# RWKV6 in a four-layer hybrid: the value rows reach all keys by transfers from DRAM, not by matmuls

## The chip, the cores and the metric

The kernel runs on one core of a Trainium2 chip. The metric is the time of one execution on the device, in microseconds (us); lower is better. All data are float32.

## What is computed

The input x is 4 sequences of 1024 tokens with 256 channels. Four residual layers follow one another, each on a layer norm of x: a retention layer, a mixture of experts (8 experts, 2 for each token), an RWKV6 layer, and the same mixture of experts again. The change is in the RWKV6 layer, cut here to its core (16 heads of 16 channels; `r_`, `k_`, `v_`, `w_` are projections of token-shifted mixes of x):

```python
ww = time_decay + jnp.tanh(xw @ td_w1) @ td_w2
w = jnp.exp(-jnp.exp(ww))
def step(state, rkvw):
    r_t, k_t, v_t, w_t = rkvw
    a = k_t[..., :, None] * v_t[..., None, :]
    y = jnp.einsum('bhk,bhkv->bhv', r_t, state + u[None, :, :, None] * a)
    new_state = w_t[..., :, None] * state + a
    return (new_state, y)
_, ys = jax.lax.scan(step, state0, (r_, k_, v_, w_))
# then: norm of y within each head, times silu(xg @ Wg), times Wo, added to x
```

## The kernel before

**Stages.** From 0 to about 350 us retention runs together with the start of the first routing, to about 672 us the tiles of the first mixture of experts (two halves of the tokens, 39 tiles each), from 686.8 to 1345 us the RWKV6 loop, and then the tiles of the second mixture. The orders of TensorE, ScalarE, VectorE and GpSimd in and after the loop are those of the program, written out by hand; the order of SP, which issues nearly all plain transfers, comes from a scheduler.

**The loop.** A block is 512 tokens; there are eight, and two blocks in a row make one sequence. Channels lie on partitions, tokens along the free axis, so that the recurrence over tokens is one scan instruction. The 256 channels are two groups g of 128 partitions (8 heads x 16 keys). The state of a head is 16 keys x 16 values; each scan handles one value index for all keys of a group. `step(j, n, ...)` treats block j and step n from 0 to 7, where n stands for g and a quarter i of the value indices (g, i = divmod(n, 4)); a step makes two runs, h = 0 and 1, of two value indices q each. "Run (n, h)" below means that one.

A run, before:
- `fill` (L916): two products on TensorE with a 0/1 matrix `pick` copy v of each head to the partitions of its 16 keys, into the PSUM tile `w_vb` (two buffers).
- `run`: VectorE multiplies `w_vb` by k in place (L939, 128x1024), then makes two scans (L941, 128x512) with w from `w_wT`, into `w_s` (six buffers). Between the two scans stand single VectorE instructions of other work: `root`, `gated`, `added`, `bonus` for neighbouring blocks, and `m.biased` (L506) of the second mixture's router. GpSimd then multiplies `w_s` by r (L949).
- `sums` (L972), one step later: TensorE adds up over the keys; after four steps ScalarE copies the result (L977).

Around the runs stand, by hand-written tables (`amid`, `late`, `uses`, `given`): the preparation of the next block (`mix`, `deltas` with its products L841 and its mixes on VectorE L851 or GpSimd L854 and L855, `decay`, `decay2`, `projected`), and the norm, gate and output of the block before. At the end of step 0 of blocks 2 to 7 the router's logits for a finished block follow (`logits`: four ScalarE instructions L487, transposes, products L502), and L506 takes them in the middle of run (1, 0). Block 5 also has the routing itself (L528 to L633), blocks 6 and 7 the sends of routed rows (L641, GpSimd's indirect transfers). In blocks 0 and 1 `join` (L759) adds the first mixture's results to x.

At step 1 of the last block all expert weights of the second mixture are loaded into the room that the RWKV6 inputs leave (`load_w1`, `load_w2`, L1228 and L1234; 16 transfers).

Of the kernel before, what the change touches and what calls it, by code (L numbers as in the profile page):

```python
# [36 lines left out]
F32 = mybir.dt.float32  # L37
I32 = mybir.dt.int32
AF = mybir.ActivationFunctionType
# [43 lines left out]

O_PICK = 0
O_SEL = O_PICK + 4 * P
O_SUM = O_SEL + 4 * 32
# [17 lines left out]
def hybrid_kernel(  # L104
# [670 lines left out]
    def rwkv(pi, w):  # L775

        st = [dict() for _ in range(NBLK)]

        def half(where, name, bufs=2):
# [86 lines left out]
        def decay2(j):  # L868

            d = st[j]  # L870
            wT = d["wT"] = full(pcs, "w_wT")
            for m in range(KC):
                wp = psum([P, BLK], "w_wp")
                mm(wp, lhsT=w["td_w2"][:, m * P : (m + 1) * P], rhs=d["tw"][:64, :],
                   start=True, stop=True)
                ew = half(pi, "w_ew", 1)
                nc.scalar.activation(ew, wp, AF.Exp, bias=vec[:, m, V_DECAY : V_DECAY + 1])
                nc.scalar.activation(wT[:, m, :], ew, AF.Exp, scale=-1.0)

        def projected(j, n, f):  # L880
            d = st[j]
            o = d[n] = full(pct if n == "g" else pcs, f"w_{n}T")
            for m in range(KC):
                pp = psum([P, BLK], "w_pp")
                for c in range(KC):
                    mm(pp, lhsT=w[n][:, c, m * P : (m + 1) * P], rhs=d["xf", f][:, c, :],
                       start=(c == 0), stop=(c == KC - 1))
                if n == "g":
                    nc.scalar.activation(o[:, m, :], pp, AF.Silu)
                else:  # L890
                    nc.scalar.copy(o[:, m, :], pp)
# [15 lines left out]

        def fill(j, n, h, among=()):


            d = st[j]
            g, i = divmod(n, 4)
            vb = d["vb", n, h] = pvb.tile([P, 2, BLK], F32, name="w_vb", tag="w_vb", bufs=2)
            for q in range(2):
                rows = slice(32 * (2 * h + q), 32 * (2 * h + q) + 32)
                mm(vb[:, q, :], lhsT=w["pick"][rows, i, :], rhs=d["v"][rows, g, :],  # L916
                   start=True, stop=True)
                for f in among[q::2]:
                    f()

# [12 lines left out]
        def run(j, n, h, between=()):  # L933


            d = st[j]
            g, i = divmod(n, 4)
            vb, s = d["vb", n, h], d["s", n, h]
            nc.vector.tensor_mul(vb, vb, d["k"][:, g, :].unsqueeze(1).to_broadcast([P, 2, BLK]))  # L939
            for q in range(2):  # L940
                nc.vector.tensor_tensor_scan(  # L941
                    s[:, q, 1 : BLK + 1], d["wT"][:, g, :], vb[:, q, :],
                    0.0 if j % NB == 0 else st[j - 1]["carry"][:, n, 2 * h + q : 2 * h + q + 1],
                    ALU.mult, ALU.add,
                )
                if q == 0:
                    for f, *a in between:
                        f(*a)
            nc.gpsimd.tensor_mul(  # L949
                s[:, :, 0:BLK], s[:, :, 0:BLK],  # L950
                d["r"][:, g, :].unsqueeze(1).to_broadcast([P, 2, BLK]),
            )
# [83 lines left out]
        def both(j, parts):  # L1036
            products, mixed = deltas(j, parts)
            for f in products:
# [11 lines left out]
            [],  # L1050
            [(0, decay2), (0, projected, "v", 2), (0, projected, "k", 1),
             (0, both, [(4, 0), (4, 1)])],
# [13 lines left out]
            0: [(1, mix, 0)],  # L1066
            1: [(0, projected, "g", 4)],
            2: [(1, mix, 1)],
# [3 lines left out]
            6: [(1, projected, "v", 2)],  # L1072
            7: [(1, projected, "r", 3)],
        }
# [6 lines left out]
            5: [(-1, out_part, 0)],  # L1081
            6: [(-1, out_part, 2), (0, centre, 0), (2, turn)],
            7: [],
# [23 lines left out]
        def step(j, n, middle):  # L1107
            def filled(jn, nn, h):
                parts = given.get((n, h)) if j + 1 < NBLK else None
                products, mixed = deltas(j + 1, parts) if parts else ((), None)  # L1110
                if jn < NBLK:
                    fill(jn, nn, h, products)
                if mixed:
                    mixed()

            following = (j, n + 1) if n < 7 else (j + 1, 0)
            if j == 0 and n == 0:
                for h in range(2):
                    ready(0, 0, h)
                fill(0, 0, 0)  # L1120
            run(j, n, 0, at(uses[n], j) + middle)
            filled(j, n, 1)
            do(amid[n], j)
            run(j, n, 1)
            filled(*following, 0)
            if following[0] < NBLK:
                for h in range(2):
                    ready(*following, h)
            do(late[n], j)
            if n > 0:  # L1130
# [47 lines left out]
    def rwkv_rest(w):  # L1178
# [9 lines left out]

        w["pick"], w["sel"] = cols(core, O_PICK, P, 4), cols(core, O_SEL, 32, 4)
        w["sum"], w["centre"] = cols(core, O_SUM, P), cols(after, O_CEN, P)  # L1190
# [33 lines left out]

    def load_w1(where):
        w1a = where.tile([P, E, KC, DFF], F32, name="w1a")
        for e in range(E):
            nc.sync.dma_start(out=w1a[:, e, :, :], in_=w1[e].rearrange("(k p) n -> p k n", p=P))  # L1228
        return w1a

    def load_w2(where):
        w2a = where.tile([P, E, KC, C], F32, name="w2a")
        for e in range(E):
            nc.sync.dma_start(out=w2a[:, e, :, :], in_=w2[e].rearrange("(k p) n -> p k n", p=P))  # L1234
        return w2a

# [28 lines left out]
    for i in range(CHUNKS):  # L1265
        step(i)
        if i == 4:
            w1a = load_w1(pw1)
        if 5 <= i < 5 + 2 * 10:
# [29 lines left out]
    pw1b = pool("pw1b", "right")  # L1299
    w2a = load_w2(pw1b)  # L1300
    px = pool("px", "right")
# [37 lines left out]

    pct, pcs, pvb = pool("pct", "right"), pool("pcs", "right"), banks("pvb")  # L1340
    rwkv_rest(w)
# [17 lines left out]
    for j in range(NBLK):  # L1359
        for n in range(8):  # L1360
# [3 lines left out]
            if j == NBLK - 1 and n == 1:  # L1364
                pi.release()
                pw2 = pool("pw2")
                w1a, w2a = load_w1(pw2), load_w2(pw2)
    finish(0)
    pvb.release()
    pcs.release()  # L1370
# [58 lines left out]
def constants():  # L1429
# [21 lines left out]
    m = c[:, A_CORE:]  # L1451
    head, part = i % GH, i // GH % 4
    r = np.arange(32)
    for j in range(4):
        m[:, O_PICK + j * P : O_PICK + (j + 1) * P] = (
            (part == j)[:, None] & (head[:, None] == i[None, :] // D))
        m[:, O_SEL + j * 32 : O_SEL + (j + 1) * 32] = (
# [57 lines left out]
```

## Time and profile before

| | us |
|---|---|
| three timed executions | 1681.85, 1684.58, 1669.92 (median 1681.85) |
| the profiled execution, its own time | 1675.26 |
| its span, first to last instruction | 1672.2 |
| busy in the span: TensorE, VectorE, GpSimd, ScalarE | 1455.9, 1003.9, 924.7, 592.4 |
| mean granted TensorE clock | 0.915 |

In profile lines a group names its source line, engine, operation, output <- inputs, shape and count, then busy time and the mean duration in ns, then the idle time of its engine ahead of it and what ended that. A timeline line begins with start and duration in us. PEld is TensorE's weight load, POOL is GpSimd, DVE VectorE, ACT ScalarE, SP the engine that issues transfers.

### The profile page before, as it was taken

The page shows a single profiled execution, that of the slowest core. Times are in us where ns is not written, and L with a number is a line of the kernel's source. Part 1 is how long each engine was busy: PE and PEld are TensorE (multiplying, and loading weights), DVE is VectorE, ACT ScalarE, POOL GpSimd, SP SyncE. Part 2 cuts the span into 40 slices and gives each one's busy share as a digit, 9 for nine tenths or more (in the row PEclk, how much of TensorE's full clock was granted, in tenths as well). Part 3 has the DMA queues.
Part 4 walks back from the last instruction along what each step waited for, and adds up shares of the span by engine and source line. Part 5 has one row for each costly group of instructions (what it writes and reads, how often), then busy time and mean ns, then how long its engine had stood idle before and what let it go on. Part 6 is the DMA issues. An engine that isn't in the chain of part 4 may idle for free. (4 is left out here: it accounts for less than half of the span.)

```text
span 1672.2 us, 21968 instructions
## 1 busy us (share of the span) xinstructions
PE 1455.9 (87%) x7312; PEld 754.5 (45%) x7312; DVE 1003.9 (60%) x1874; ACT 592.4 (35%) x1428; POOL 924.7 (55%) x879
## 2 busy tenths in 40 slices
PE   6999998868988999999999899978878768989993
PEld 4666665635555555322333333423323235555662
DVE  6676656314423433499889798899877923423534
ACT  2343434323443333333333433323233233443331
POOL 4233324632564343699979697867697822564331
PEclk9999999878999999989989898978888767999997
DMA  8921211132334421112100000000001410333625
GB/s 298 338 77 52 64 39 61 59 117 76 96 122 137 136 67 53 39 25 39 26 1 1 0 1 1 1 1 1 13 26 63 143 55 29 110 120 125 205 92 176
DMA packets 88332, 128.91 MB, mean 77 GB/s; under 512 B 9152, under 2 KB 70432, under 8 KB 88224
## 3 DMA queue, kind: packets, MB, share of 16 engines
q1 hardware_dynamic: 70368, 85.82, 16.7%
q0 software_dynamic: 17856, 41.70, 8.0%
q8 instruction: 62, 1.02, 0.3%
q14 instruction: 46, 0.38, 0.1%
HBM read 75.42 MB, written 52.06 MB: 76 GB/s over the span
## 5 line engine op out<-in xcount | busy, mean ns | idle before, releaser
L949 POOL TENSOR_TENSOR w_s<-w_s,w_rT 128x1024 f32<-128x1024 f32 x128 | 304.5, 2393 | 87.8 <-DVE w_s L941 87.2
L709 POOL DMA_INDIRECT y_all<-m_y,m_to x156 | 150.8, 967 | 330.3 <-ACT m_xt L664 189.7
L669 PE MATMUL m_hp<-w1a,m_xt 128*128 x624 | 309.5, 620 | 10.9 <-ACT m_xt L664 10.9
L675 DVE TENSOR_TENSOR m_a<-m_hp,m_sg 128x256 f32<-128x256 f32 x156 | 66.1, 424 | 350.3 <-ACT m_sg L673 308.9
L916 PE MATMUL w_vb<-w_vT,core_c 32*128 32x512 f32 x512 | 160.5, 711 | 45.3 <-DVE w_s L941 45.2
L703 PE MATMUL m_op<-w2a,m_aT 128*128 x624 | 165.2, 388 | 22.3 <-ACT m_y L708 20.0
L939 DVE TENSOR_TENSOR w_vb<-w_vb,w_kT 128x1024 f32<-128x1024 f32 x128 | 155.8, 1217 | 43.3 <-PE w_vb L916 43.0
L941 DVE TENSOR_TENSOR_SCAN w_s<-w_wT,w_carry,w_vb 128x512 f32<-128x512 f32 x128 | 159.8, 1272 | 7.9 <-DVE w_vb L939 0.5
L941 DVE TENSOR_TENSOR_SCAN w_s<-w_wT,w_vb 128x512 f32<-128x512 f32 x128 | 151.6, 1211 | 7.6 <-DVE w_vb L939 0.5
L669 PEld LDWEIGHTS m_hp<-w1a,m_xt 128*128 128x128 f32 x624 | 111.8, 199 | 92.8 <-issue 79.9
L641 POOL DMA_INDIRECT xg_all<-m_row,m_at x128 | 124.7, 974 | 51.3 <-issue 28.0
L703 PEld LDWEIGHTS m_op<-w2a,m_aT 128*128 128x128 f32 x624 | 107.7, 193 | 37.8 <-ACT m_y L708 27.4
L708 ACT ACTIVATE m_y<-m_op,m_share 128x256 f32<-128x256 f32 x156 | 73.8, 473 | 142.7 <-PE m_op L703 81.8
L673 ACT ACTIVATE m_sg<-m_hp 128x256 f32<-128x256 f32 x156 | 59.9, 384 | 171.6 <-PE m_hp L669 140.4
L916 PEld LDWEIGHTS w_vb<-w_vT,core_c 32*128 32x128 f32 x512 | 42.1, 201 | 149.3 <-DVE w_s L941 84.0
L298 POOL TENSOR_TENSOR a_t<-a_t,a_t 128x512 f32<-128x512 f32 x32 | 41.1, 1284 | 116.0 <-DVE a_t L297 93.7
L855 POOL TENSOR_TENSOR w_xf<-w_xf,w_xT 128x512 f32<-128x512 f32 x80 | 86.0, 1091 | 4.2 <-DVE w_xf L851 0.4
L696 PEld LDWEIGHTS m_atp<-cst,m_a 128*128 128x128 f32 x312 | 44.1, 144 | 89.7 <-issue 72.7
L328 DVE TENSOR_TENSOR a_pt<-a_sp,ret_c 128x2048 f32<-128x2048 f32 x32 | 73.1, 2285 | 15.9 <-PE a_sp L325 15.8
L972 PE MATMUL w_yp<-w_s,core_c 128*32 128x512 f32 x512 | 78.0, 663 | 5.0 <-POOL w_s L949 5.0
L664 ACT COPY m_xt<-m_xtp 128x256 f32<-128x256 f32 x156 | 56.9, 366 | 45.2 <-PE m_xtp L660 44.5
L660 PE MATMUL m_xtp<-cst,m_xg 128*128 128x128 f32 x312 | 62.6, 285 | 11.7 <-DMA m_xg<-xg_all 11.5
(226 smaller groups left out, 2523.4 us busy)
## 6 DMA issues: line engine op xcount, KB each, us to landing
m_xg<-xg_all SPq DMA_DIRECT2D x36, 520.0 KB
tab<-in_rope SPq DMA_DIRECT2D x32, 512.0 KB
m_back<-y_all SPq DMA_DIRECT2D x48, 256.0 KB
xg_all<-zero SPq DMA_DIRECT2D x18, 520.0 KB
w1a<-in_w SPq DMA_DIRECT2D x16, 512.0 KB
res<-in_x SPq DMA_DIRECT2D x8, 512.0 KB
w2a<-in_w SPq DMA_DIRECT2D x16, 256.0 KB
res<-y_all POOLq DMA_DIRECT2D x8, 512.0 KB
```

What stands on the lines that cost most here:

```text
L328: nc.vector.tensor_mul(pts[i].rearrange("p j n t -> p (j n) t"), sp.rearrange("p j n t -> p (j n) t"), causal.unsqueeze(1).to_broadcast([P ...
L641: nc.gpsimd.indirect_dma_start(out=xg_views[self.half][2 * i + n][:, :], out_offset=bass.IndirectOffsetOnAxis(ap=self.at[n][:, i : i + 1], ...
L669: mm(hp, lhsT=self.xt[j][:, c, :], rhs=w1a[:, bass.ds(self.ev[j], 1), c, :].rearrange("p o n -> p (o n)"), start=(c == 0), stop=(c == KC - 1))
L703: mm(op, lhsT=self.aT[j][:, c, :], rhs=w2a[:, bass.ds(self.ev[j], 1), c, :].rearrange("p o n -> p (o n)"), start=(c == 0), stop=(c == KC - 1))
L708: nc.scalar.activation(y, op, AF.Copy, scale=self.share[g][:, i : i + 1])
L709: nc.gpsimd.indirect_dma_start(out=y_views[self.half][j][:, :], out_offset=bass.IndirectOffsetOnAxis(ap=self.to[g][:, i : i + 1], axis=0), ...
L855: nc.gpsimd.tensor_add(xf, xf, d["now"][:, c, :])
L916: mm(vb[:, q, :], lhsT=w["pick"][rows, i, :], rhs=d["v"][rows, g, :], start=True, stop=True)
L939: nc.vector.tensor_mul(vb, vb, d["k"][:, g, :].unsqueeze(1).to_broadcast([P, 2, BLK]))
L941: nc.vector.tensor_tensor_scan(s[:, q, 1 : BLK + 1], d["wT"][:, g, :], vb[:, q, :], 0.0 if j % NB == 0 else st[j - 1]["carry"][:, n, 2 * h ...
L949: nc.gpsimd.tensor_mul(s[:, :, 0:BLK], s[:, :, 0:BLK], d["r"][:, g, :].unsqueeze(1).to_broadcast([P, 2, BLK]),)
L972: mm(d["yp", g][32 * q : 32 * q + 32, :], lhsT=w["sel"][:, i, :], rhs=d["s", n, q // 2][:, q % 2, 0:BLK], start=False, stop=(i == 3), skip ...
```

## The change

v of a block is written to DRAM, and each run's `w_vb` is read from there, broadcast to the keys' partitions by the transfer itself. `w_vb` moves from PSUM to SBUF and gets three buffers. In the four PSUM banks that it leaves lies `w_wk`: w and k of one channel group at a time (half the channels), two buffers. The second exponential of w moves from `decay2` to the new `factors`, which also copies k there; `factors` for group 1 is called in step 1, for group 0 of the next block in step 7. `fill` no longer takes turns with the mixing products, which now come together as `both`. `fill` for a run is issued two runs ahead. The expert loads of the last block are spread over its steps 2 to 7. The matrix `pick` and its place in the constants go.

```diff
+        vds = [[tc.dram_tile([P, 2 * BLK], F32, name=f"v_all{n}{g}") for g in range(KC)]
+               for n in range(2)]
...
         def decay2(j):
             d = st[j]
-            wT = d["wT"] = full(pcs, "w_wT")
+            ew = d["ew"] = full(pcs, "w_ew", 1)
             for m in range(KC):
...
-                ew = half(pi, "w_ew", 1)
-                nc.scalar.activation(ew, wp, AF.Exp, bias=vec[:, m, V_DECAY : V_DECAY + 1])
-                nc.scalar.activation(wT[:, m, :], ew, AF.Exp, scale=-1.0)
+                nc.scalar.activation(
+                    ew[:, m, :], wp, AF.Exp, bias=vec[:, m, V_DECAY : V_DECAY + 1])
...
-            o = d[n] = full(pct if n == "g" else pcs, f"w_{n}T")
+            o = d[n] = full(pct if n == "g" else pcs, f"w_{n}T", 1 if n == "k" else 2)
...
-        def fill(j, n, h, among=()):
-            d = st[j]
+        def factors(j, g):
+            d = st[j]
+            wk = d["wk", g] = pwk.tile([P, 2, BLK], F32, name="w_wk", tag="w_wk", bufs=2)
+            nc.scalar.activation(wk[:, 0, :], d["ew"][:, g, :], AF.Exp, scale=-1.0)
+            nc.scalar.copy(wk[:, 1, :], d["k"][:, g, :])
+
+        def store(j):
+            for g in range(KC):
+                for q in range(4):
+                    rows, cols = vds[j % 2][g][q // 2 * 64 : q // 2 * 64 + 64, :], q % 2 * BLK
+                    nc.sync.dma_start(
+                        out=rows[:, cols : cols + BLK].rearrange("(r u) t -> r u t", u=2),
+                        in_=st[j]["v"][32 * q : 32 * q + 32, g, :].unsqueeze(1).to_broadcast(
+                            [32, 2, BLK]),
+                    )
+
+        def fill(j, m):
+            d = st[j]
+            n, h = divmod(m, 2)
             g, i = divmod(n, 4)
-            vb = d["vb", n, h] = pvb.tile([P, 2, BLK], F32, name="w_vb", tag="w_vb", bufs=2)
-            for q in range(2):
-                rows = slice(32 * (2 * h + q), 32 * (2 * h + q) + 32)
-                mm(vb[:, q, :], lhsT=w["pick"][rows, i, :], rhs=d["v"][rows, g, :],
-                   start=True, stop=True)
-                for f in among[q::2]:
-                    f()
+            vb = d["vb", n, h] = pcs.tile([P, 2, BLK], F32, name="w_vb", tag="w_vb", bufs=3)
+            row = 64 * h + 2 * GH * i
+            nc.sync.dma_start(
+                out=vb.rearrange("p q t -> p (q t)"),
+                in_=vds[j % 2][g][row : row + 2 * GH, :].unsqueeze(1).to_broadcast(
+                    [2 * GH, D // 2, 2 * BLK]),
+            )
...
-            vb, s = d["vb", n, h], d["s", n, h]
-            nc.vector.tensor_mul(vb, vb, d["k"][:, g, :].unsqueeze(1).to_broadcast([P, 2, BLK]))
+            vb, s, wk = d["vb", n, h], d["s", n, h], d["wk", g]
+            nc.vector.tensor_mul(vb, vb, wk[:, 1:2, :].to_broadcast([P, 2, BLK]))
             for q in range(2):
                 nc.vector.tensor_tensor_scan(
-                    s[:, q, 1 : BLK + 1], d["wT"][:, g, :], vb[:, q, :],
+                    s[:, q, 1 : BLK + 1], wk[:, 0, :], vb[:, q, :],
...
-            [(0, decay2), (0, projected, "v", 2), (0, projected, "k", 1),
+            [(0, decay2), (0, projected, "v", 2), (0, store), (0, projected, "k", 1),
...
-            1: [(0, projected, "g", 4)],
+            1: [(0, projected, "g", 4), (0, factors, 1)],
...
-            7: [(1, projected, "r", 3)],
+            7: [(1, projected, "r", 3), (1, factors, 0)],
...
-            6: [(-1, out_part, 2), (0, centre, 0), (2, turn)],
+            6: [(1, store), (-1, out_part, 2), (0, centre, 0), (2, turn)],
...
         def step(j, n, middle):
-            def filled(jn, nn, h):
-                parts = given.get((n, h)) if j + 1 < NBLK else None
-                products, mixed = deltas(j + 1, parts) if parts else ((), None)
-                if jn < NBLK:
-                    fill(jn, nn, h, products)
-                if mixed:
-                    mixed()
-
-            following = (j, n + 1) if n < 7 else (j + 1, 0)
+            def filled(m):
+                if j + m // 16 < NBLK:
+                    fill(j + m // 16, m % 16)
+
+            def mixing(h):
+                if (n, h) in given and j + 1 < NBLK:
+                    both(j + 1, given[n, h])
+
             if j == 0 and n == 0:
                 for h in range(2):
                     ready(0, 0, h)
-                fill(0, 0, 0)
-            run(j, n, 0, at(uses[n], j) + middle)
-            filled(j, n, 1)
-            do(amid[n], j)
-            run(j, n, 1)
-            filled(*following, 0)
+                factors(0, 0)
+                for m in range(2):
+                    filled(m)
+            for h in range(2):
+                filled(2 * n + h + 2)
+                run(j, n, h, at(uses[n], j) + middle if h == 0 else ())
+                mixing(1 - h)
+                if h == 0:
+                    do(amid[n], j)
+            following = (j, n + 1) if n < 7 else (j + 1, 0)
...
-    pct, pcs, pvb = pool("pct", "right"), pool("pcs", "right"), banks("pvb")
+    pct, pcs, pwk = pool("pct", "right"), pool("pcs", "right"), banks("pwk")
...
             if j == NBLK - 1 and n == 1:
                 pi.release()
                 pw2 = pool("pw2")
-                w1a, w2a = load_w1(pw2), load_w2(pw2)
+                w1a, w2a = room(pw2)
+            if j == NBLK - 1 and n > 1:
+                some = range((n - 2) * E // 6, (n - 1) * E // 6)
+                load(w1a, w1, some)
+                load(w2a, w2, some)
```

More of the change, by code (lines that the diff above doesn't have):

```diff
@@ L82 @@
 N_AVG = P
-O_PICK = 0
-O_SEL = O_PICK + 4 * P
+O_SEL = 0
 O_SUM = O_SEL + 4 * 32
@@ L1187, in cols @@
             return t if k is None else t.rearrange("p (k n) -> p k n", k=k)
-        w["pick"], w["sel"] = cols(core, O_PICK, P, 4), cols(core, O_SEL, 32, 4)
+        w["sel"] = cols(core, O_SEL, 32, 4)
         w["sum"], w["centre"] = cols(core, O_SUM, P), cols(after, O_CEN, P)
@@ L1223, in hybrid_kernel, with room, load @@
     ph = pool("ph")
[L1225 to L1235, printed above, removed]
+    def room(where):
+        return (where.tile([P, E, KC, DFF], F32, name="w1a"),
+                where.tile([P, E, KC, C], F32, name="w2a"))
+    def load(t, src, experts=range(E)):
+        for e in experts:
+            nc.sync.dma_start(out=t[:, e, :, :], in_=src[e].rearrange("(k p) n -> p k n", p=P))
     ctx.enter_context(
@@ L1267, in hybrid_kernel @@
         if i == 4:
-            w1a = load_w1(pw1)
+            w1a = pw1.tile([P, E, KC, DFF], F32, name="w1a")
+            load(w1a, w1)
         if 5 <= i < 5 + 2 * 10:
@@ L1299, in hybrid_kernel @@
     pw1b = pool("pw1b", "right")
-    w2a = load_w2(pw1b)
+    w2a = pw1b.tile([P, E, KC, C], F32, name="w2a")
+    load(w2a, w2)
     px = pool("px", "right")
@@ L1366, in hybrid_kernel @@
                 pw2 = pool("pw2")
-                w1a, w2a = load_w1(pw2), load_w2(pw2)
+                w1a, w2a = room(pw2)
[3 more added lines that the diff above has]
+                load(w2a, w2, some)
     finish(0)
-    pvb.release()
+    pwk.release()
     pcs.release()
@@ L1451, in constants @@
     m = c[:, A_CORE:]
-    head, part = i % GH, i // GH % 4
+    head = i % GH
     r = np.arange(32)
     for j in range(4):
-        m[:, O_PICK + j * P : O_PICK + (j + 1) * P] = (
-            (part == j)[:, None] & (head[:, None] == i[None, :] // D))
         m[:, O_SEL + j * 32 : O_SEL + (j + 1) * 32] = (
```

## The prediction

> **What bounds the kernel now.** I read first where the touched tiles live in time, then the busy times of that stretch by block, then what VectorE and GpSimd wait for, and last the timeline around one block boundary. The tiles `w_vb` and `w_s` appear from 686.8 to 1344 us, so the change concerns 658 of 1672.2 us: eight blocks, each with 16 runs (one multiply L939, two scans L941, then GpSimd's multiply L949). The page's costliest groups give the prices:
>
> ```profile
> L949 POOL TENSOR_TENSOR w_s<-w_s,w_rT 128x1024 f32<-128x1024 f32 x128 | 304.5, 2393 | 87.8 <-DVE w_s L941 87.2
> L916 PE MATMUL w_vb<-w_vT,core_c 32*128 32x512 f32 x512 | 160.5, 711 | 45.3 <-DVE w_s L941 45.2
> L939 DVE TENSOR_TENSOR w_vb<-w_vb,w_kT 128x1024 f32<-128x1024 f32 x128 | 155.8, 1217 | 43.3 <-PE w_vb L916 43.0
> ```
>
> The answer by windows, two middle blocks and the sum of the loop (columns: stretch, length, then busy time of PE, weight load, VectorE, ScalarE, GpSimd, granted clock, DMA share, GB/s):
>
> ```profile
> 920.00:1002.00 82.00, 75.19 (x296) 28.02 (x296) 70.17 (x83) 29.67 (x59) 65.86 (x48) 0.92 0.00 0
> 1002.00:1084.00 82.00, 76.24 (x305) 28.67 (x305) 70.16 (x83) 32.49 (x72) 66.91 (x60) 0.92 0.00 1
> 686.80:1345.00 658.20, 575.98 (x2203) 204.19 (x2202) 566.75 (x652) 220.83 (x481) 538.83 (x428) 0.88 0.09 23
> ```
>
> No engine fills a block: VectorE works 70 of 82 us, GpSimd 66. DMA is idle in the middle blocks. What stops VectorE in the loop, from the waits (13.26 us of the first line stand before the first run, so 30 us are in the loop):
>
> ```profile
> DVE w_vb L939 <- PE w_vb L916: 43.0, 28, 13.3
> DVE m_logit L506 <- PE m_lp L502: 23.4, 6, 5.4
> ```
>
> The timeline of one boundary shows that the two are coupled:
>
> ```profile
> 987.60 1.23 DVE L939 TENSOR_TENSOR w_vb<-w_vb,w_kT 128x1024 f32<-128x1024 f32 x1 [1.62 <-PE w_vb L916]
> ...
> 994.20 2.35 POOL L949 TENSOR_TENSOR w_s<-w_s,w_rT 128x1024 f32<-128x1024 f32 x1
> ...
> 997.86 1.13 PE L916 MATMUL w_vb<-w_vT,core_c 32*128 32x512 f32 x4
> ...
> 999.97 1.06 PE L972 MATMUL w_yp<-w_s,core_c 128*32 128x512 f32 x8
> 1001.13 0.58 ACT L977 COPY w_y<-w_yp 128x512 f32<-128x512 f32 x1 [2.57 <-PE w_yp L972]
> 1001.61 2.08 ACT L487 ACTIVATE m_xn<-res,m_shift,m_rstd 128x256 f32<-128x256 f32 x4
> ...
> 1007.83 0.19 DVE L506 TENSOR_TENSOR m_logit<-m_lp,bias 128x32 f32<-128x32 f32 x1 [4.14 <-PE m_lp L502]
> ```
>
> GpSimd's last multiply of a block ends at 996.55; the sums that read it start only at 999.97, because two fills and other products stand ahead of them in TensorE's order. Then ScalarE, the router's products and L506 follow, and VectorE stands in the middle of a run until 1007.83. So a block's period runs L506, first half set by VectorE (GpSimd waits for it), second half set by GpSimd (no wait over 0.7 us from 954 to 996), then this chain.
>
> [...] L939 (one PSUM, one SBUF input) keeps 1203 to 1233 ns beside a busy GpSimd, while the routing's L622 on 128x7, both inputs in SBUF, took 2265 ns. The change keeps one input in PSUM, only the other one. [...] the trace's chain has 3.62 us for a 520 KB `m_xg`, and a stretch of weight loading (1300 to 1310) moves 346 GB/s. [...]
>
> **The change, part by part.**
> Fills out of TensorE: 512 matmuls, 160.5 us of its busy time. TensorE is not the end of a block, so the worth is in its order. (a) First half: taking block 926 to 1008, VectorE waited 2.22 us at 934.96 (fill behind the eight `w_g` products), and for `w_dp` 0.82, 0.53, 0.41 (products interleaved with fills): 3.9 us, and GpSimd, which waited 3.81, 3.11 and 1.34 us for VectorE there, moves up by the same. (b) Chain: the sums can start at 996.55 + 0.25 in place of 999.97; their 7.86 us to L506 stay: 3.2 us. VectorE saves 1.62 more at 987.60, so it reaches L506 at about 998.2 and waits 2.5 us. Sum 7.1 us a block: 81.7 becomes 74.6, which still holds VectorE's 70.2, 2.5 of L506 and 2 of small gaps.
>
> By block:
> - 2, 3, 4 (three periods): 3 x 7.1 = 21.3.
> - 0 and 1 have no L506, and GpSimd is 65.8 of 71 and 77.3 of 81 us busy: of 4.7 and 3.4 us of fill waits I take 2 each, 4 together.
> - 5 carries the routing (L506 to L506 109.2 us, VectorE 96.9 busy): only its fill and `w_dp` waits, 0.90 + 0.52 + 0.82 + 1.62 = 3.9.
> - 6: GpSimd is full with the sends; the sums move up 2.7 us and one wait of 0.99 goes: 3.5, less than the sum since VectorE must arrive too.
> - 7: see loads below: -1.
>
> New transfers: 128 reads of 512 KB (67.1 MB) and 64 stores of 128 KB (8.4 MB), on SP's queue. A read costs SP 0.33 us (row `tab`), and lands after 3.6 us (from `m_xg`); 67.1 MB over some 620 us is 108 GB/s, a third of the 340 seen. Three buffers: read m+2 starts when run m-1 has ended, and has two runs, at least 2 x 3.7 = 7.4 us. Hidden with 3.8 us to spare. [...] I take 3.6.
>
> Store at a boundary: VectorE ends run (6,0) at 977.9, the two copies of v end 979.4 and 981.1. In SP's order the first store stands ahead of the read for run (7,1), which leaves at 979.8 and lands by 983.5, needed at 986. The eight stores are issued by 982.4 [...]; the read behind them lands near 988.5 and is needed at 991.9. Hidden by 3.4 us; without that cover each late microsecond counts in seven boundaries.
>
> ScalarE: 16 exponentials only move, 16 copies of 0.58 us are new, and eight table loads of 1.28 us (one elsewhere goes): 19 us on an engine 221 of 658 us busy. The pair for a new block stands behind the two copies of r; ready about 991, needed 991.9: nothing, at worst 1 us a block. The single buffer for k and the shared `w_ew` are reused in ScalarE's own order or after L894 of the block before: nothing.
>
> VectorE: same instructions in the same order. The multiply now has L1026's operands (SBUF and PSUM in, SBUF out), which takes 661 ns for 512 elements: at most 1.32 us for 1024, about 1.2 with one fixed part, so between 2 us less and 13 us more over 128 runs; I take no change. The scans only swap which input is in PSUM: 0, and I allow 0.03 us a scan either way (8 us).
>
> Start: v's stores stand behind the `w_o` and `w_ln` loads, issued to 679.5; the first read lands near 687, the factors follow the copies of `w_xT` (to 687.7) by 1.2: first run 689, was 688.05: -1. `core_c` shrinks by 256 KB, under other waits: 0.
>
> Expert loads: in SP's order the first one stands ahead of the read for run (2,0) of the last block, and waits for the last `w_g` products. Before they ended at 1288.97, 7.5 us after L506; without fills about 5.5, so this read, behind 512 KB, lands at L506 + 11.2 where the run began at L506 + 8.65: 2.5 us lost, 1.5 won elsewhere: the -1 above. The loads themselves (6.3 MB over 55 us beside the reads) stay under 230 GB/s and end before the loop.
>
> Sum: 21.3 + 4 + 3.9 + 3.5 - 1 - 1 = 30.7 us. After the loop nothing changes. Against the profiled execution's 1675.26 us: 1644.6. The median of the three timed runs is 6.6 us above it, which would give 1651; I take 1648, between the two.
>
> **Rivals.**
> 1. Forecast: transfers hidden, 1648, own range 1632 to 1662. Chance 0.56.
> 2. Partly exposed: boundaries and the last block are late by 2 to 5 us each, since stores, reads and v's late copy follow in one queue. For it: the spare is only 3 to 4 us and SP waits in order. 8 x 3 = 24 us given back: 1672. Chance 0.19.
> 3. Transfers become the bound (slower): all 16 engines read one 64 KB piece of HBM, each row eight times. A run takes 658 / 128 = 5.1 us, so below 75.5 MB / 658 us = 115 GB/s the queue sets the loop. [...] For it: no such read in the trace[...]. Chance 0.19.
> 4. More than forecast: TensorE, less loaded, gets a higher clock than the loop's mean of 0.88, the router's products shorten and the scans keep their time: another 25 us: 1623. Chance 0.06.
>
> Measurement tells a kernel from no change at about 1%. Rivals 1, 4 and a fifth of 2 give faster 0.64; the rest of 2 and the edge of 1, same 0.15; 3 and the tail of 2, slower 0.21. The range 1620 to 1700 leaves out most of 3.
>
> **What would show it.** Right: VectorE's waits for `w_vb` under 10 us in the loop, now from DMA; L939 near 1.20 us and the scans unchanged; periods of L506 near 75 us in blocks 2 to 4; the sums within 1 us of GpSimd's last multiply; DMA share 0.3 to 0.4. Wrong: waits of several us on `v_all` reads in every run (3) or only at the first run of each block (2); scans or L949 longer by more than 0.05 us; GpSimd idle no less than 119 us of the loop.

## The result, and the profile after

The changed kernel takes 1688.13 us (median of 20 runs, 1676.98 to 1696.71), the kernel before 1678.47 us (20 runs); the ratio is 1.0055, interval 1.0037 to 1.0074. It is slower by some 9 us where some 30 us of gain were forecast. The profiled execution has a span of 1688.7 us against 1672.2.

Of these 16.5 us, 10.1 lie before the loop: its first multiply starts at 698.12 in place of 688.05. The upstream stage, whose code is the same, ended 8.7 us later in this execution; 1.3 us are left for the change (the first multiply waits 15.43 us for its read, where it waited 13.26 for fills). That stage scatters: in the profiled executions of n1 to n4 below, on one chip, it ended between 655.4 and 664.7 us. The rest I take from the times of L505 (L506 before), which end each stretch of the loop (a period runs from one such addition for the logits to the next; the three steady ones are those of blocks 2 to 4, the routing is in block 5):

| us | first scan to first logits | three steady periods | routing period | next | last |
|---|---|---|---|---|---|
| before | 156.9 | 239.7 | 109.1 | 86.4 | 80.5 |
| after | 157.1 | 244.2 | 105.4 | 84.7 | 89.3 |

So the loop up to the last logits loses 7.9 us (what follows wins 1.5): the steady blocks, which were to win 21 us, lose 4.5, and the last period loses 8.7. The page's groups of after that answer to those of before:

```profile
L967 POOL TENSOR_TENSOR w_s<-w_s,w_rT 128x1024 f32<-128x1024 f32 x128 | 304.2, 2394 | 92.3 <-DVE w_s L959 88.6
L957 DVE TENSOR_TENSOR w_vb<-w_vb,w_wk 128x1024 f32<-128x1024 f32 x128 | 153.9, 1202 | 37.2 <-DMA w_vb<-v_all 20.9
```

GpSimd's multiply and VectorE's cost what they cost before. The fills are gone, and VectorE's idle time ahead of its multiply has fallen only from 43.3 to 37.2 us. The same stretches by windows (columns as before: two middle blocks, then the loop):

```profile
937.60:1019.40 81.80, 71.48 (x233) 27.14 (x233) 69.70 (x81) 31.53 (x61) 65.52 (x49) 0.83 0.43 116
1019.40:1100.70 81.30, 72.51 (x233) 27.21 (x233) 68.30 (x82) 32.42 (x69) 65.71 (x57) 0.81 0.44 117
698.10:1361.00 662.90, 523.34 (x1685) 189.82 (x1685) 565.51 (x652) 235.85 (x501) 534.93 (x426) 0.81 0.52 133
```

About 500 products less, and TensorE's busy time falls only from 576 to 523 us: its granted clock falls from 0.88 to 0.81, and some of the fills had run beside other products (shown further below). VectorE's waits in and around the loop, first the one line of before that the first of them is to be held against:

```profile
DVE w_xf L851 <- PE w_dp L841: 8.0, 11, 0.9
```

```profile
DVE w_xf L852 <- PE w_dp L842: 22.3, 10, 3.6
DVE w_vb L957 <- DMA w_vb<-v_all: 20.9, 7, 15.4
DVE res L224 <- PE w_op L219: 13.7, 6, 6.8
DVE m_logit L505 <- PE m_lp L501: 10.8, 5, 5.4
DVE w_vb L957 <- issue: 9.4, 1, 9.4
DVE w_vb L957 <- ACT w_wk L913: 6.9, 4, 2.7
```

The first line of after is new in size: VectorE's waits for the mixing products have grown from 8.0 to 22.3 us, in pieces of up to 3.6. (Those for the output products `w_op`, 13.7 against 5.1 us, have grown too; they are 14.5 us in p3, the fastest version below, and 10.4 us in the kernel before without fills, so they are not what sets the slow version apart.) The timeline behind the logits of one block shows why:

```profile
1009.04 2.34 POOL L967 TENSOR_TENSOR w_s<-w_s,w_rT 128x1024 f32<-128x1024 f32 x1
...
1011.43 1.07 PE L990 MATMUL w_yp<-w_s,core_c 128*32 128x512 f32 x8
...
1019.32 2.07 PE L842 MATMUL w_dp<-w_m,tm_w2a 32*128 32x512 f32 x2
1019.43 0.19 DVE L505 TENSOR_TENSOR m_logit<-m_lp,bias 128x32 f32<-128x32 f32 x1 [1.31 <-PE m_lp L501]
...
1021.43 0.69 ACT L854 ACTIVATE w_xf<-w_dp,vec 128x512 f32<-128x512 f32 x1 [4.85 <-PE w_dp L842]
...
1022.17 2.07 PE L842 MATMUL w_dp<-w_m,tm_w2a 32*128 32x512 f32 x2 [0.78 <-ACT w_xf L854]
...
1024.35 0.75 DVE L852 SCALAR_TENSOR_TENSOR w_xf<-w_dp,vec,w_sx 128x512 f32<-128x512 f32 x1 [3.60 <-PE w_dp L842]
```

The second mixing product waits until ScalarE has read the first. The built program, in which each tile has its place, says why: both lie in the same PSUM bank, in all five blocks that have a logits stage ahead of them. The three banks of the pool's tag `mm` are handed out when the program is built, and with the fills gone they are handed out in another sequence. In the loop of the kernel before no two `mm` tiles that follow each other on TensorE share a bank; in the changed one 12 pairs do. VectorE's L852 begins 4.92 us after the logits' add, where it began 2.20 us after it before (1007.83 to 10.03).

The last block shows the other wait. The load of expert weights that stands ahead of the read in SP's order goes into room that the g projection's inputs held, so it left only when these products had ended (at 1298.78):

```profile
1298.85 0.40 SPq L1253 DMA_DIRECT2D w1a<-in_w  x1
1299.35 0.51 SPq L933 DMA_DIRECT2D w_vb<-v_all  x1
...
1305.22 1.22 DVE L957 TENSOR_TENSOR w_vb<-w_vb,w_wk 128x1024 f32<-128x1024 f32 x1 [9.40 <-issue]
```

### The profile page after: what moved, and what is told of

Read it like the earlier page. It is cut to its first block, busy times and chain, and to the rows that moved or that the text cites. A ratio compares the mean times of both kernels' runs of the same rounds, so it can differ in the third digit from the quotient of the medians.

```text
span 1688.7 us, 21332 instructions
## 1 busy us (share of the span) xinstructions
PE 1418.5 (84%) x6800; PEld 747.9 (44%) x6800; DVE 1002.8 (59%) x1874; ACT 608.8 (36%) x1451; POOL 925.2 (55%) x879
## 5 line engine op out<-in xcount | busy, mean ns | idle before, releaser
L702 PE MATMUL m_op<-w2a,m_aT 128*128 x624 | 165.2, 388 | 13.7 <-ACT m_y L707 11.2
L957 DVE TENSOR_TENSOR w_vb<-w_vb,w_wk 128x1024 f32<-128x1024 f32 x128 | 153.9, 1202 | 37.2 <-DMA w_vb<-v_all 20.9
L959 DVE TENSOR_TENSOR_SCAN w_s<-w_wk,w_carry,w_vb 128x512 f32<-128x512 f32 x128 | 160.2, 1275 | 7.8
L959 DVE TENSOR_TENSOR_SCAN w_s<-w_wk,w_vb 128x512 f32<-128x512 f32 x128 | 152.0, 1215 | 7.4
L707 ACT ACTIVATE m_y<-m_op,m_share 128x256 f32<-128x256 f32 x156 | 73.8, 473 | 133.4 <-PE m_op L702 85.4
L990 PE MATMUL w_yp<-w_s,core_c 128*32 128x512 f32 x512 | 91.0, 711 | 10.9 <-POOL w_s L967 10.7
L842 PE MATMUL w_dp<-w_m,tm_w2a 32*128 32x512 f32 x128 | 75.5, 837 | 17.3 <-DVE w_cen L1044 7.4
L856 POOL TENSOR_TENSOR w_xf<-w_xf,w_xT 128x512 f32<-128x512 f32 x80 | 86.1, 1091 | 4.2 <-DVE w_xf L852 0.4
L697 DVE COPY m_aT<-m_atp 128x256 f32<-128x256 f32 x156 | 64.9, 416 | 5.2 <-PE m_xtp L659 2.9
```

What stands on the lines that cost most here:

```text
L702: mm(op, lhsT=self.aT[j][:, c, :], rhs=w2a[:, bass.ds(self.ev[j], 1), c, :].rearrange("p o n -> p (o n)"), start=(c == 0), stop=(c == KC - 1))
L707: nc.scalar.activation(y, op, AF.Copy, scale=self.share[g][:, i : i + 1])
L842: mm(dp, lhsT=wt[rows, c * P : (c + 1) * P], rhs=m[rows, :], start=True, stop=True)
L856: nc.gpsimd.tensor_add(xf, xf, d["now"][:, c, :])
L957: nc.vector.tensor_mul(vb, vb, wk[:, 1:2, :].to_broadcast([P, 2, BLK]))
L959: nc.vector.tensor_tensor_scan(s[:, q, 1 : BLK + 1], wk[:, 0, :], vb[:, q, :], 0.0 if j % NB == 0 else st[j - 1]["carry"][:, n, 2 * h + q ...
```

## The experiments

The theories at this point: (A) the transfers' traffic lowers TensorE's clock; (D) the clock falls because the fills are gone; (E) the shared bank eats the gain; (G) so does the load ahead of the read; against them that the fills never cost anything. All ratios are to the kernel before, run beside each experiment on the same chip; three chips were used (for n1 to n4, for o1 to o4, for p1 to p4), and its medians there were 1647 to 1649 us. An amount in us that stands beside a ratio is worked out from the ratio.

**n1, without the reads.**

```diff
-            vb = d["vb", n, h] = pcs.tile([P, 2, BLK], F32, name="w_vb", tag="w_vb", bufs=3)
+            vb = d["vb", n, h] = pcs.tile([P, 2, BLK], F32, name="w_vb", tag="w_vb", bufs=2)
+            if j or m:
+                return
+            vb = w["vs"] = pcs.tile([P, 2, BLK], F32, name="w_vs", tag="w_vs", bufs=1)
...
-            nc.vector.tensor_mul(vb, vb, wk[:, 1:2, :].to_broadcast([P, 2, BLK]))
+            nc.vector.tensor_mul(vb, w["vs"], wk[:, 1:2, :].to_broadcast([P, 2, BLK]))
```

> The changed kernel without its transfers: v's first rows are read once, and every run multiplies those (the values of v in the later runs are left out; the stores to DRAM, w and k in PSUM, and the order of the instructions stay). Theory A (the traffic lowers the granted TensorE clock of the loop from 0.88 to 0.81 and eats the gain): the clock is back at 0.88, the loop shrinks from 663 to some 630 us and the kernel runs at 1650 to 1658. Rival B (the transfers cost only by landing late: 9.4 us in the last block and 5.5 us in the others): the clock stays near 0.81, the time is 1672 to 1675. Rival C (nothing in the transfers costs anything): within 4 us of the changed kernel's 1688.

Ratio 0.9881 (0.9854 to 0.9909). The time fell, but the clock of the loop is 0.79 at 35 GB/s: theory A's reason is wrong. The edit also moved the banks (3 pairs share one, in place of 12), so it prices nothing alone; o3 comes nearer.

**n2, the kernel before without fills.**

```diff
-            vb = d["vb", n, h] = pvb.tile([P, 2, BLK], F32, name="w_vb", tag="w_vb", bufs=2)
+            vb = d["vb", n, h] = pvb.tile([P, 2, BLK], F32, name="w_vb", tag="w_vb", bufs=1)
+            once = j == 0 and n == 0 and h == 0
+            if once:
+                vb = w["vs"] = pvb.tile([P, 2, BLK], F32, name="w_vs", tag="w_vs", bufs=1)
...
-                mm(vb[:, q, :], lhsT=w["pick"][rows, i, :], rhs=d["v"][rows, g, :],
-                   start=True, stop=True)
+                if once:
+                    mm(vb[:, q, :], lhsT=w["pick"][rows, i, :], rhs=d["v"][rows, g, :],
+                       start=True, stop=True)
...
-            nc.vector.tensor_mul(vb, vb, d["k"][:, g, :].unsqueeze(1).to_broadcast([P, 2, BLK]))
+            nc.vector.tensor_mul(vb, w["vs"], d["k"][:, g, :].unsqueeze(1).to_broadcast([P, 2, BLK]))
```

> The kernel before without its fill matmuls: one filled buffer is kept in PSUM and every run multiplies it into another (the values of v in the later runs are left out; no transfer is added, w and k stay in SBUF). It bounds what taking the fills out of TensorE's order can give. Theory A (the fills held up the mixing products and the chain to the logits, about 7 us in a block): 1645 to 1655, clock of the loop 0.88 or more. Rival B (the blocks are set by GpSimd and the chain through the sums, fills or not): 1673 to 1682 at clock 0.88. Rival D (the clock falls because the fills are gone, whatever the transfers do): clock of the loop 0.81 to 0.84 and a time of 1665 to 1680.

Ratio 0.9869 (0.9840 to 0.9897), 21.6 us of gain: the fills were worth that much, and the rival that they cost nothing is out. But the clock is theory D's:

```profile
672.20:1303.10 630.90, 517.38 (x1686) 190.63 (x1684) 571.98 (x647) 219.65 (x478) 533.77 (x425) 0.81 0.09 23
```

**n3, the kernel before with as much traffic.**

Behind each of GpSimd's multiplies stands a transfer more:

```diff
+            nc.sync.dma_start(
+                out=extra_out[(2 * n + h) % 3].rearrange("p (q t) -> p q t", q=2),
+                in_=s[:, :, 0:BLK],
+            )
```

> The kernel before, whole, with one extra transfer of 512 KB after each run: the multiplied states are also written to a scratch tile in DRAM. As many bytes as the changed kernel's reads move, at the same pace, and nothing waits for them but the states' buffers. Theory A (traffic lowers the granted clock): the clock of the loop falls from 0.88 to 0.81 to 0.84, and the time rises by 12 to 30 us. Rival D (the clock has to do with TensorE's own work alone): clock 0.88, time within 5 us of the kernel before.

Ratio 1.0005 (0.9988 to 1.0022), and the window of its loop:

```profile
678.60:1328.50 649.90, 571.15 (x2190) 201.17 (x2188) 565.08 (x647) 220.29 (x478) 533.78 (x425) 0.88 0.36 125
```

Five times the bytes and the same clock. Its stretches (154.8, 239.0, 109.4, 86.1, 80.9) are also those of the kernel before within 2.1 us, on the chip of n1 to n4. Its extra transfers write where the changed kernel's read; that reads don't lower the clock either is seen in n1, which has none (0.79, where the changed kernel with them had 0.81). With the kernel before, n2 and n4 below this is a table of two by two: with fills 0.88 at 23 and at 125 GB/s, without them 0.81 at 23 and 0.82 at 139. So theory A falls and D stands.

**n4, the two products parted.**

```diff
-            (1, 1): [(1, 0), (0, 0)],
+            (1, 1): [(0, 0), (1, 0)],
```

> The changed kernel with the two mixing products behind the logits given in the other order (VectorE's ahead of ScalarE's). The buffers then fall so that the two products lie in two PSUM banks; in the changed kernel they share one, and the second waits until ScalarE has read the first, 3.5 us in which VectorE stands. Theory E (these waits cost the five blocks with logits about 3 us each): VectorE's waits for w_dp fall from 22 to 8 us and the time by 9 to 15 us, to 1673 to 1679. Rival F (VectorE's wait there is slack that the next wait, for GpSimd or for the sums, takes over): the waits fall, the time stays within 4 us of 1688.

With this order the two products lie in two banks, and in the loop only 2 pairs share one. Ratio 0.9955 (0.9933 to 0.9977), 7 us under the kernel before where the changed kernel was 9 us over it, so the bank is worth some 16 us. VectorE's waits and the timeline at the place shown above:

```profile
DVE w_xf L852 <- PE w_dp L842: 8.6, 10, 1.1
```

```profile
985.55 2.08 PE L842 MATMUL w_dp<-w_m,tm_w2a 32*128 32x512 f32 x4
985.66 0.19 DVE L505 TENSOR_TENSOR m_logit<-m_lp,bias 128x32 f32<-128x32 f32 x1 [1.50 <-PE m_lp L501]
...
987.73 0.75 DVE L852 SCALAR_TENSOR_TENSOR w_xf<-w_dp,vec,w_sx 128x512 f32<-128x512 f32 x1 [0.75 <-PE w_dp L842]
```

L852 begins 2.07 us after the logits' add, 2.20 us before the change. That VectorE's product now stands first is not what helps: the four instructions of the two products start in pairs and end together, in the 2.08 us that one product alone took in the changed kernel (2.07), and ScalarE and VectorE read them at the same time. The steady periods are 75.1, 77.6 and 75.1 us.

**o4, the shared bank in the kernel before.**

```diff
+            bank = [psum([P, BLK], "w_dp")] if shared else None
...
-                dp = psum([P, BLK], "w_dp")
+                dp = bank[0] if shared else psum([P, BLK], "w_dp")
...
+            if shared:
+                def second():
+                    mixed()
+                    dps.clear()
+                    product(*parts[1])
+                return [lambda: product(*parts[0]), second], mixed
...
-                products, mixed = deltas(j + 1, parts) if parts else ((), None)
+                products, mixed = deltas(j + 1, parts, j > 1 and (n, h) == (1, 1)) if parts else ((), None)
```

> The kernel before, fills and all, with one edit: in the five blocks with a logits stage the two mixing products behind it are written into the same PSUM tile, the second when ScalarE has read the first, as the changed kernel's buffers fall. Theory E (the shared bank alone costs what made the changed kernel slow): VectorE's w_dp waits rise from 8 to 20 us or more, and the time rises by 10 to 16 us, ratio 1.006 to 1.010. Rival F (with the fills in TensorE's order the wait hides behind the fills' own): within 4 us, ratio under 1.0025.

Ratio 1.0123 (1.0087 to 1.0159): 20 us for one shared bank in five blocks, more than expected. Its waits:

```profile
DVE w_vb L946 <- PE w_vb L923: 52.4, 27, 13.1
DVE m_logit L506 <- PE m_lp L502: 21.9, 6, 5.1
DVE w_xf L852 <- PE w_dp L842: 21.5, 11, 3.6
```

The w_dp waits are those of the changed kernel (21.5 against 22.3), and here the fills queue behind the waiting product too (52.4 against 43.0 us). Its steady periods are 82.6, 84.8 and 83.3 us. Theory E is shown from both sides: parting the products in the changed kernel wins 16 us, and putting them in one bank in the kernel before costs 20.

**o1, the parted products and the loads on ScalarE's queue.** Besides n4's edit:

```diff
-                load(w1a, w1, some)
-                load(w2a, w2, some)
+                load(w1a, w1, some, nc.scalar)
+                load(w2a, w2, some, nc.scalar)
```

> The changed kernel with the two mixing products parted in banks (as in n4) and the sixteen loads of expert weights of the last block issued by ScalarE in place of SP, so that no read of v stands behind a load that waits for TensorE. Theory G (that load held up the reads by 9.8 us, and all of it was on the path): VectorE's wait in the last block goes, the last steady period of the logits falls from 86.2 to 77 to 80 us, and the ratio to the kernel before falls from 0.9955 to 0.989 to 0.992. Rival H (GpSimd or the loads' own landing at the loop's end takes over): the wait goes, the ratio stays at 0.994 to 0.997.

Ratio 0.9868 (0.9831 to 0.9904); VectorE's long wait in the last block is gone, and the last period falls from n4's 86.2 to 78.8 us, as theory G had it. The ratio fell by more (14 us) than this period did (7.5 us), and the three steady periods are longer than n4's (235.7 against 227.8 us), so o1 alone does not price the loads.

**o2, earlier factors and an earlier start besides.**

```diff
-            6: [(1, projected, "v", 2)],
-            7: [(1, projected, "r", 3), (1, factors, 0)],
+            6: [(1, factors, 0), (1, projected, "v", 2)],
+            7: [(1, projected, "r", 3)],
...
```

At the start v and its first four stores also move ahead of `decay2`, and the other four behind the first reads.

> As o1, and besides: w and k of the next block's first half go to PSUM one step earlier (ahead of the v and r projections, for VectorE's 6.8 us of waits for w_wk), and at the start v is projected ahead of the decays and the first read is issued between the stores of the first and of the second half of the channels (for the 15.3 us at the loop's start). Theory I (each of these waits is on the path): w_wk waits under 2 us, start wait 11 to 13 us, a further 5 to 8 us, ratio 0.984 to 0.988. Rival J (the w_wk waits are slack in front of GpSimd's sums): start alone pays, ratio within 0.003 of o1.

Ratio 0.9911 (0.9877 to 0.9945): no better than o1, and not told apart from it. The `w_wk` waits in the loop are gone, but the waits for the logits rise from 10.7 to 16.5 us and the periods between logits are o1's within 0.3 us: they were slack, as rival J had it. At the start the wait is 14.9 us, now for `w_wk`, where o1 waited 16.3 us for its read: one lateness replaced the other.

**o3, no reads and parted banks.** n1 with n4's edit.

> As n1 (v's rows read once, the values of v in the later runs left out, stores kept), but with the two mixing products parted in banks as in n4. Against n4 and o1 it prices the 127 reads alone. Theory K (the reads cost only what waits show, 5 us behind the late loads and some 2 us elsewhere): the same as o1 within 0.003, ratio 0.988 to 0.992. Rival L (the reads slow the other engines' accesses or the clock without any wait for them): 0.978 to 0.985, and GpSimd's or VectorE's mean durations fall.

Ratio 0.9885 (0.9853 to 0.9917), o1's within the intervals, each 5 to 6 us to either side. So the 127 reads cost nothing that these runs can tell from zero once nothing stands ahead of them. The banks are not quite the same here: in n4, o1 and p3 the two halves of the last block's g projection still share one, in o3 no pair of the loop does, and its last period is 75.9 us against o1's 78.8.

**p1 to p3, the parts on one chip.** p1 is the changed kernel, p2 has o1's loads alone, p3 is o1 again.

> The changed kernel as it stands, on the chip of the next three, so that their differences to it need not go through another chip. If the parts add up as n4 and o1 said (banks 16.5 us, loads 14 us), it stands at 1.005 of the kernel before, some 18 to 20 parts in a thousand above p3. If o1's gain was the chip's or the hour's, p3 stands nearer.

> The changed kernel with the expert loads issued by ScalarE and nothing else: the two mixing products still share a bank. Theory G (the loads' wait, 9.4 us in the last block, is on the path by itself): 8 to 14 us under p1, ratio 0.997 to 1.000. Rival M (the gain of o1 over n4 is not the loads' but the scatter of the two profiled series): 0 to 4 us under p1, ratio 1.003 to 1.006.

> The kernel of o1 once more, beside p1 and p2. Theory (banks and loads add up, and together they are the whole of what hid the gain): ratio 0.984 to 0.991, the best version so far. Of its profile: the steady blocks fall at 75 us as in n4 or at 78.4 us as in o1, which have the same instructions on TensorE; either would show that the difference lies in the granted clock of one execution.

Ratios 1.0039 (1.0020 to 1.0058), 0.9997 (0.9976 to 1.0019) and 0.9841 (0.9816 to 0.9867). The loads alone give 7 us, somewhat less than the wait of 9.2 us in the last block of p1; the bank alone, n4 against p1, 14; both together 33 (29.6 by the medians, 1655.74 and 1626.18 us). Some 8 to 12 us more than the sum stay open. They are not seen in the profiled executions: from the first multiply of the loop to the end p1 takes 968.2 us, n4 953.0, o1 951.9 and p3 948.9, which is 15 us for the bank, 1 to 4 for the loads and 19 for both. Nor is p1's profiled execution a middling one: at 1638.0 us it is the lowest of its runs, all others of which took over 1649 us, while p3's five lie within 7 us. Scatter ahead of the loop, as in the section on the result, would be enough for the rest, but no run shows that it is the cause. p3 is the fastest version here, 26 us under the kernel before by the ratio, 22.7 by the medians. Its steady periods are 77.7, 77.7 and 78.0 us, o1's 78.4, 79.0 and 78.4, n4's 75.1, 77.6 and 75.1, with the same TensorE instructions there: in the blocks compared, the g projection behind the logits took 6.47 us in o1 and 5.16 in n4, and the granted clock in the 6 us from the logits' add on was 0.50 and 0.59.

**p4, more work for TensorE between the logits' products.**

```diff
+                if self.layer == 1:
+                    for c in range(KC):
+                        mm(t[:, 256:384], lhsT=tT[:, c, i * P : (i + 1) * P], rhs=ident,
+                           start=True, stop=True)
```

> The kernel of p3, and between the narrow products of the logits (8 columns) of the second mixture eight more products of 128 columns into an unused part of the same bank, which nothing reads. Theory N (TensorE's clock halves behind the logits because the array has had little to do, and the mixing products and the g projection pay for it): the two mixing products fall from 2.07 to 1.2 us, the g projection from 6.2 to 4 to 5 us, and the time by 2 to 10 us or, with the added products' own 2 us a block, not at all (within 4 us). Rival O (the clock does not answer to such work): the spell stays, and the time rises by 8 to 15 us, since the logits wait for the added products.

Ratio 0.9998 (0.9976 to 1.0020), some 26 us above p3 by the ratio (22.4 by the medians), more than either theory allowed. The clock around one block's logits, p3 first (logits' products, mixing products, g projection in two parts), then p4 (the extended logits stage in three parts, mixing products, g projection in two parts):

```profile
900.20:902.90 2.70, 2.67 (x17) 2.63 (x16) 2.46 (x3) 0.61 (x2) 2.05 (x1) 0.69 0.68 193
902.90:904.90 2.00, 2.00 (x5) 0.50 (x4) 1.38 (x2) 0.00 (x0) 0.31 (x1) 0.50 0.02 2
904.90:907.50 2.60, 2.60 (x5) 1.18 (x4) 2.29 (x3) 1.97 (x2) 2.60 (x2) 0.50 0.69 192
907.50:910.00 2.50, 2.50 (x6) 1.10 (x5) 2.50 (x3) 0.60 (x1) 2.42 (x3) 0.89 0.05 10
```

```profile
913.40:915.40 2.00, 2.00 (x11) 2.00 (x10) 1.87 (x3) 0.59 (x1) 1.97 (x1) 0.50 0.66 195
915.40:917.40 2.00, 2.00 (x12) 2.00 (x11) 0.49 (x1) 0.00 (x0) 0.00 (x0) 0.50 0.29 68
917.40:920.40 3.00, 3.00 (x14) 2.88 (x14) 0.00 (x0) 0.00 (x0) 0.00 (x0) 0.50 0.00 0
920.40:922.40 2.00, 2.00 (x5) 0.51 (x4) 1.38 (x2) 0.00 (x0) 0.23 (x1) 0.50 0.00 0
922.40:925.40 3.00, 3.00 (x6) 1.33 (x5) 2.61 (x3) 1.97 (x2) 3.00 (x2) 0.50 0.64 175
925.40:928.40 3.00, 3.00 (x8) 1.29 (x7) 2.87 (x4) 0.85 (x2) 2.92 (x4) 0.84 0.00 0
```

In the block shown the added products ran at half clock themselves and made the spell longer; VectorE's waits for the logits in the loop rose from 10.6 to 24.3 us. So theory N falls, and rival O has the direction and the reason. In both kernels the full clock came back only after 3 to 4 us of the g projection's 512-column products (begun at 904.93 and 922.52): some 3.1 us in p3 and 3.8 in p4, an estimate from the mean clocks of the last windows, 0.89 and 0.84, taken as 0.50 up to the return and 1.00 from there.

## Why the prediction was wrong

**Step (b), the sums: right.** They start at 1011.43, 0.05 us after GpSimd's last multiply ended, where 3.42 us lay between before the change; from there to the logits' add it takes 8.0 us against 7.86.

**Step (a), the first half: the step that failed.** "VectorE waited 2.22 us at 934.96 (fill behind the eight `w_g` products), and for `w_dp` 0.82, 0.53, 0.41 (products interleaved with fills): 3.9 us, and GpSimd ... moves up by the same." It took the waits for the mixing products to go with the fills that stand between these products. They did not go. In the changed kernel a shared bank made them longer: GpSimd's last multiply ends 73.8 us after the logits' add of the block before, where it was 70.5 us. The 3.3 us lost in the first half are the 3.4 us won by the sums, so the period stayed at 82 us. The banks could have been read from the built program before the run.

Without the shared bank the step still falls short. In n4 the multiply ends at 69.3 us, 1.1 us earlier than before the change and not 3.9. Of the four waits only the 2.22 us for a fill is gone; the two for `w_dp` are 0.69 and 0.95 us where they were 0.82 and 0.53, and the fourth, 0.41, was for `w_varp` (L1008) and not for `w_dp` at all. In the whole loop the waits for `w_dp` are 8.6 us in n4 and were 8.0 before. The timeline of before shows the reason:

```profile
1007.72 1.22 PE L916 MATMUL w_vb<-w_vT,core_c 32*128 32x512 f32 x1
1007.73 1.22 PE L841 MATMUL w_dp<-w_m,tm_w2a 32*128 32x512 f32 x1
1007.74 1.22 PE L916 MATMUL w_vb<-w_vT,core_c 32*128 32x512 f32 x1
1007.74 1.22 PE L841 MATMUL w_dp<-w_m,tm_w2a 32*128 32x512 f32 x1
```

Each of these products uses 32 rows of the array, and the two fills and the two mixing products ran at the same time, within 0.02 us of one another. In this place the fills cost the mixing products next to nothing, and taking them out could give next to nothing.

**By block.** Without the bank the steady blocks are worth less than the 7.1 us each: n4's three take 227.8 us and p3's 233.4, against 239.7 before, 12 and 6 in place of 21. The forecast took 81.7 us for each, the longest of the three (79.9, 81.7, 78.1), and an unchanged clock. The cleanest measure of this is n2 against n3, on one chip and without the shared bank in four of the five blocks: the five stretches of the table are shorter by 5.0, 2.7, 6.0, 3.0 and 4.6 us, together 21.3, about its whole gain of 21.6, and the steady blocks have only 2.7 of them. Blocks 0 and 1 were worth 5 (151.5 in p3 against 156.9; 4 forecast), the routing block 6 (103.2 against 109.1; 3.9 forecast). In p3 the sixth won 0.3 us of 3.5, and the last, with the loads on ScalarE's queue, 1.9. That p3 as a whole comes to 23 to 26 of the 30.7 us forecast is therefore partly luck: the terms are not those of the sum.

**Expert loads.** The mechanism was named and mis-sized. The run behind the load was to begin 2.5 us later after the logits' add than before the change; it began at 14.5 us where it was 8.65, 5.8 us later, with 9.4 us of waiting. The last g products were counted as ending 5.5 us after the logits' add. Their second half began at 1295.00, 0.69 us late for ScalarE's read of the first half, which had the same bank, and took 3.78 us at clock 0.50: they ended 8.0 us after the add at 1290.74.

**The clock.** The forecast held it at 0.88, and rival 4 let it rise. It fell, and n2 shows that this follows from taking the fills out (0.81 where the kernel before had 0.88). The windows show half the rate and the full one (0.50 in p4 from 913.40 to 925.40, and 1.00 ahead of the logits, from 905.40 to 911.40) and the 3 to 4 us of wide products until the return. They do not show what makes the clock fall: in p3 it fell between 900.20 and 902.90 (mean 0.69), when TensorE was busy for 2.67 of 2.70 us, as it had been for 1.71 of the 1.90 us before at 1.00. Why it falls more without the fills is not shown, and no run isolates what the lower clock costs. n2 gained 21.6 us in spite of it.

**Right as it stands:** transfers hidden (o3; 5.5 us of waits for reads in the loop of after, each up to 2.2), though a read took SP 0.51 us where 0.33 was counted and the DMA share was 0.52, not 0.3 to 0.4; L957 at 1202 ns; scans at 1.22 to 1.28 us; start 1.3 us late for 1. The `w_wk` waits were 1.05 to 2.75 us in four blocks where "at worst 1 us" was allowed, but o2 shows them as slack. "GpSimd idle no less than 119 us", the sign of failure, came true: 662.9 - 534.9 = 128 us. Rival 2, with reads late by 2 to 5 us at each boundary, was right for the last block alone, where the read was late for a load and not for stores. Rival 3, the transfers as the bound, was the author's estimate, and no read of this kind stood in the trace of before; it was not it: the loop of after moved 133 GB/s, over the 115 below which the queue was to set the loop.

## What to carry to other kernels

Taking instructions out of an engine's order can change which buffers the remaining ones get: compare which tiles share a bank or a buffer around the edit in the built program before adding up what goes. A gain on the chain from one block to the next is only worth what the other half of the block doesn't lose, so a period should be followed from one fixed instruction to the next with its offsets. Products that use different rows of the array may already run at the same time (four of 32 rows each began within 0.02 us here), so look at their start times before counting what the removal of one gives the other. And where work leaves TensorE, don't hold its clock fixed in the sum: here it fell from 0.88 to 0.81.

## What the runs showed of the hardware that I had not expected

TensorE's clock in the loop depended on its own work and not on traffic: 0.88 with the fills at 23 and 125 GB/s, 0.79 to 0.83 in the loops without them at 23 to 139 GB/s. TensorE can be busy in every record and stay at half clock: in p4 from 913.4 to 925.4 us, through 8-, 128- and 512-column products, with weight loads almost all the time until 920.4. The same TensorE instructions in the same order gave steady periods of 75.1 us in one profiled execution (n4) and of 78.4 in another (o1), and in the block compared the half-clock spell lasted longer in the slower one. Products on 32 rows each ran two or four at a time, in the time of one: 2.07 us for one mixing product in the changed kernel (at 1019.32), 2.08 for two in p3 (at 902.93), both at clock 0.50, and 1.22 us each for four that began within 0.02 us in the kernel before (at 1007.72), at 0.50 too. And reads of 512 KB that take each row of DRAM eight times kept pace with a run each 5 us, 133 GB/s over the loop, at no cost that o3 could tell from zero.
